# A first scan whose rows come half by DMA, half by TensorE, with stores on another queue

## The chip, the cores and the metric

The kernel runs on one core of a Trainium2 chip. The metric is the time of one execution on the device, in microseconds (us). Shapes and data are fixed. PE is TensorE (PEld its weight loads), DVE VectorE, ACT ScalarE, POOL GpSimd and SP SyncE, which here only issues DMAs.

## The reference, cut to what matters

The input is x of 32 sequences x 256 tokens x 256 channels and a condition of 32 x 512. A selective scan is followed by two layers of windowed attention and a gated feed-forward block; x is added at the end. The scan part is what the change touches:

```python
xr, gate = jnp.split(x @ W_in.T, 2, axis=-1)
xr = xr + t_emb[:, None, :]
xc = silu(causal_conv4(xr) + b_conv)
xn = layernorm(xc) * ln_g + ln_b                  # 512 channels
Bm, Cm, dt = jnp.split(xn @ W_xproj.T, 3, axis=-1)  # 16 states each
Ad = 1.0 + tanh(dt @ W_dt.T + b_dt) * 0.01 * (-tanh(A_log))
Bd = Bm * jnp.minimum(norm(xn), 1.0)
h = clip(h * ad[:, :, None] + bd[:, :, None] * xt[:, None, :], -10, 10)  # each token
yt = einsum('bd,bdh->bh', ct, h)
y = ys + D * xn
out = (y * silu(gate)) @ W_out.T
```

Here h has 16 states x 512 channels for each sequence, and a step depends on the step before.

## The kernel before

All data is fp32, apart from a mask and a scratch in bf16. The 32 sequences are worked in four groups of eight (`GB`). `program` runs the scan of group 0 by itself, then, for each group, attention and feed-forward of that group (`blocks`) side by side with the scan of the next group; `side_by_side` (L61) deals out `SCAN_PIECES` pieces of the scan over the main pieces. The last group has no scan beside it.

`group_scan` (L304) keeps h as a tile of 128 partitions (16 states x 8 sequences) by 512 channels. The 256 tokens are cut in eight chunks (`NCH`) of 32 (`CH`), and a chunk in two halves of 16 tokens (`TB`), called hb. The decay is taken out of the recurrence: by running products, a step is one add with two clamps on DVE (`step`, L550). Its other operand is row t of xn, repeated for all 16 states and scaled by a per-partition beta:

- `norm_out` (L456) stores the normalised tokens, by SP, to a scratch in DRAM, `xnd`.
- `load_rows` (L536) reads two rows (`XR` = 2) of it back, each repeated 16 times over the partitions, into a tile `xrep` of 512 KB. There are three such tiles.
- `scale_row` (L541) multiplies one row in place by beta on ACT (L543).
- `step` adds it to h. There are eight h tiles.
- `read_out` (L557) contracts the states on PE with weights `ly`, four tokens into four strips of 32 columns (`NQ` = 4), into a PSUM bank `y` for each half.
- `load_skip` (L570) reads the same 16 tokens of `xnd` again, not repeated, in four DMAs into `xd`: partition 32q + 8i + b holds token 4i + q of sequence b. `skip` (L582) multiplies by D on POOL, `gated` adds y, `out_turn` transposes on PE, `out_gate` multiplies by the gate, `project_y` projects, `copy_y` evacuates on ACT and `put_y` (L648) stores to the scratch `ys`, by SP.
- `raw_turn` (L403) takes raw B, C and dt sums from a tile of 64 partitions to one of 128, in three DMAs by SP.

Order is written out as an agenda: `at(s, what, ...)` puts a piece into slot s, slot c*32 + t being that of step t of chunk c, and every slot is emitted in the order of its list. The tile framework then orders each engine's instructions and places the waits; the order in the trace is near that of the slots, not the same. [...] Seven PSUM banks (`ps_w`) are shared, in turn, by all products but y. Slots before the change, relative to a chunk's first step s0: `load_x` -46, `project` of the convolution's half -40 to -34 and of the gates 13, 16, 17, 18, `raw_turn` -23, `norm_stats` -22 and -18, `norm_out` -17 and -13, `load_rows` five slots and `scale_row` two slots ahead of a step, `read_out` four tokens at a time one or two slots after the last of them, `load_skip` 5 and 21, `skip` 9 and 25, `put_y` 42 and 44.

Of the kernel before, what the change touches and what calls it, by code (L numbers as in the profile page):

```python
# [10 lines left out]
FP = mybir.dt.float32  # L11
BF = mybir.dt.bfloat16
I32 = mybir.dt.int32
AF = mybir.ActivationFunctionType
# [5 lines left out]
P = 128  # L20
# [3 lines left out]
DI = 512  # L24
NC_ = DI // P
NS = 16
GB = 8
CH = 32
NCH = S // CH
TB = P // GB  # L30
NQ = 4
NI = TB // NQ
NJ = GB * CH // P
BJ = GB // NJ
XR = 2
TAPS = 4
HEADS = 8
DH = 64
# [14 lines left out]
def bc(ap, axis, n):  # L53

    ap = ap.unsqueeze(axis)
    shape = list(ap.shape)
    shape[axis] = n
    return ap.broadcast_to(shape)
# [15 lines left out]
def kernel(  # L74
# [29 lines left out]
    nc = tc.nc  # L104
# [23 lines left out]
    dskip_sb = loaded(d_skip.partition_broadcast(P), [P, DI], "dskip_sb")  # L128
# [8 lines left out]
    ident = const.tile([P, P], FP, tag="ident", name="ident")  # L137
    make_identity(nc, ident)

    def sums(name, n, src):  # L140
        t = const.tile([P, n], FP, tag=name, name=name)
        nc.vector.tensor_reduce(t, src, AX.X, ALU.add)
        return t
# [2 lines left out]

    st_seq = sums("st_seq", GB, ident.rearrange("p (n b) -> p b n", b=GB))
    tok_step = sums("tok_step", CH, ident.rearrange("p (b t) -> p t b", b=BJ))

    sel = const.tile([P, NJ, NS, GB], FP, tag="sel", name="sel")  # L150
    nc.gpsimd.memset(sel, 0.0)
    tok_seq = sums("tok_seq", BJ, ident.rearrange("p (b t) -> p b t", b=BJ))
    for j in range(NJ):
# [25 lines left out]
        out=mask_t[:, 0:W], in_=mask_t[:, 0:W], compare_op=ALU.is_ge, fill=MASKED_LOW,  # L179
# [3 lines left out]
        out=mask_t[:, W : 2 * W], in_=mask_t[:, W : 2 * W], compare_op=ALU.is_ge,  # L183
# [9 lines left out]
    for h in range(HEADS):  # L193
# [7 lines left out]
        out=b1g_sb[DH : DH + MREM], in_=b1[0:MREM, :, 1, len(MCH) - 1]  # L201
# [12 lines left out]
    with tc.tile_pool(name="setup", bufs=2) as setup, tc.tile_pool(  # L214
        name="setup_ps", bufs=2, space=PSUM
    ) as sps:

        for src, pos, dst in ((qk_scale, rot_c, rc_sb), (qk_scale_sw, rot_s, rs_sb)):
            tab = setup.tile([P, NW, 2, DH], FP, tag="tab", name="tab")
            nc.scalar.dma_start(out=tab, in_=pos)  # L220
            for l in range(L):
                sc = setup.tile([P, 2 * DH], FP, tag="qk_sc", name="qk_sc")
                nc.scalar.dma_start(
                    out=sc, in_=src[l].rearrange("a d -> (a d)").partition_broadcast(P)
# [39 lines left out]
        for i in range(3):  # L264
            for src, k, dst in ((wx_sb, 0, wsum), (wx0, 1, wbias)):
# [3 lines left out]
                for c in range(NC_):  # L269
# [4 lines left out]
                        start=(c == 0),  # L274
                        stop=(c == NC_ - 1),
# [7 lines left out]
    for i in range(2):  # L283
        t = const.tile([P, NI * (P + GB)], FP, tag=f"ly{i}", name=f"ly{i}")
# [3 lines left out]
    def program(ctx, exact):  # L288
        rpool = ctx.enter_context(tc.tile_pool(name="res", bufs=1, reuse_waits="tile"))
        wpool = ctx.enter_context(tc.tile_pool(name="weights", bufs=1, reuse_waits="tile"))  # L290
        sp = ctx.enter_context(tc.tile_pool(name="sp", bufs=1, reuse_waits="tile"))
# [5 lines left out]
        ap_ = ctx.enter_context(tc.tile_pool(name="at", bufs=2, reuse_waits="tile"))  # L297
        aw = ctx.enter_context(tc.tile_pool(name="aw", bufs=3, reuse_waits="tile"))
        ps_w = ctx.enter_context(tc.tile_pool(name="psw", bufs=7, space=PSUM, reuse_waits="tile"))

        def bank(pool, tag, name):
            return pool.tile([P, DI], FP, tag=tag, name=name)

        def group_scan(g, ys):  # L304
# [2 lines left out]

            b0 = g * GB  # L310
            agenda = {}
            state = {"p": one}
            ck = [{} for _ in range(NCH)]

            def at(s, what, *args):
                agenda.setdefault(s, []).append(partial(what, *args))
# [86 lines left out]
            def raw_turn(c):  # L403
                rw = sm.tile([P, 3, CH], FP, tag="rw", name="rw")
                raw = ck[c].pop("raw")
                for i in range(3):
                    nc.sync.dma_start(
                        out=rw[:, i],
                        in_=raw[i * NS : (i + 1) * NS].rearrange("n (b t) -> n b t", b=GB),
                    )  # L410
                ck[c]["rw"] = rw
# [121 lines left out]
            def rows(c):  # L533
                return ck[c]["xnd"].rearrange("(b t) d -> b t d", b=GB)

            def load_rows(c, t):  # L536
                xr = xp.tile([P, XR, DI], FP, tag="xrep", name="xrep")
                nc.sync.dma_start(out=xr, in_=bc(rows(c)[:, t : t + XR, :], 0, NS))
                ck[c]["rep", t // XR] = xr

            def scale_row(c, t):  # L541
                bx = ck[c]["rep", t // XR][:, t % XR]
                nc.scalar.activation(  # L543
                    bx, bx, AF.Copy, scale=ck[c]["beta"][:, t : t + 1]
                )

            def step(c, t):
# [20 lines left out]
                    )  # L568

            def load_skip(c, hb):  # L570
                xd = sp.tile([P, DI], FP, tag="xd", name="xd")
                for q in range(NQ):
                    t0 = hb * TB + q
                    nc.sync.dma_start(
                        out=xd[q * 32 : (q + 1) * 32],
                        in_=rows(c)[:, t0 : t0 + TB - NQ + 1 : NQ, :].rearrange(
                            "b i d -> i b d"
                        ),
                    )
                ck[c]["xd"] = xd  # L580

            def skip(c):  # L582
                nc.gpsimd.tensor_mul(ck[c]["xd"], ck[c]["xd"], dskip_sb)  # L583

            def gate_th(c, ch):
                th = sp.tile([P, GB * CH], FP, tag="th", name="th_g", bufs=2)
# [59 lines left out]
                ck[c]["yo", d] = yo  # L646

            def put_y(c, d):  # L648
                nc.sync.dma_start(
                    out=ys[:, d, :, c * CH : (c + 1) * CH], in_=ck[c].pop(("yo", d))  # L650
                )

            def start():
                h0 = hp.tile([P, DI], FP, tag="h", name="h0")
                nc.vector.memset(h0, 0.0)
                state["h"] = h0

            at(-1, start)
            for c in range(NCH):
                for t in range(CH):  # L660
                    at(c * CH + t, step, c, t)
            for c in range(NCH):
                s0 = c * CH

                for hb in range(CH // TB):
                    s = s0 + hb * TB
                    for i in range(NI):
                        at(s + 4 * i + 5, read_out, c, hb, i)
                    at(s + 19, gated, c, hb)
                    at(s + 22, out_gate, c, hb)  # L670
                    at(s + 9, skip, c)
                for ch in range(NC_):
                    at(s0 - 38 + 2 * ch, conv_in, c, ch)
                    at(s0 - 37 + 2 * ch, conv_taps, c, ch)
                    at(s0 - 35 + 2 * ch, conv_out, c, ch)
                for ch, s in enumerate((13, 16, 17, 18)):
                    at(s0 + s + 1, gate_th, c, ch)
                    at(s0 + s + 2, gate_out, c, ch)
                at(s0 - 24, raw_copy, c)
                at(s0 - 23, raw_turn, c)  # L680
                for j in range(NJ):
                    s = s0 - 24 + 4 * j
                    at(s + 2, norm_stats, c, j)
                    at(s + 4, norm_apply, c, j)
                    at(s + 5, norm_affine, c, j)
                    at(s + 7, norm_out, c, j)
                at(s0 - 11, length, c)
                at(s0 - 7, figures_in, c)
                at(s0 - 5, decays, c)
                at(s0 - 4, put_c, c, 0)  # L690
                at(s0 + 4, put_c, c, 1)
                for d in range(KM):
                    at(s0 + 41 + 2 * d, copy_y, c, d)
                    at(s0 + 42 + 2 * d, put_y, c, d)
            for c in range(NCH):
                s0 = c * CH
                at(s0 - 46, load_x, c)
                for ch in range(NC_):
                    at(s0 - 40 + 2 * ch, project, c, ch)
                for ch, s in enumerate((13, 16, 17, 18)):  # L700
                    at(s0 + s, project, c, NC_ + ch)
                at(s0 - 26, raw_sums, c)
                for j in range(NJ):
                    at(s0 - 24 + 4 * j, norm_turn, c, j)
                at(s0 - 9, figures, c)
                for t in range(CH):
                    if t % XR == 0:
                        at(s0 + t - 5, load_rows, c, t)
                    at(s0 + t - 2, scale_row, c, t)
                for hb in range(CH // TB):  # L710
                    s = s0 + hb * TB
                    at(s + 5, load_skip, c, hb)
                    at(s + 20, out_turn, c)
                for d in range(KM):
                    at(s0 + 39 + 2 * d, project_y, c, d)
# [3 lines left out]
                    what()  # L719
                yield  # L720

        SCAN_PIECES = NCH * CH + 46 + 13

        def load_res(ys, j):
            t = rpool.tile([P, KM, 2, 1 + S], FP, tag=f"res{j}", name=f"res{j}")
# [175 lines left out]
        class Attention:  # L901
# [52 lines left out]
            def sums(self, b):  # L954

                rs = bank(ps_w, "w", "rs")[:, 0:S]
                for kw in range(NW):
                    for r in range(2):
                        for i in range(HEADS // 2):
                            nc.tensor.matmul(  # L960
                                rs[32 * i : 32 * i + 32, kw * W :],
                                head_cols[:, r],
                                self.p[b, kw, i, r],
                                start=(kw == 0 and r == 0),
                                stop=(kw == NW - 1 and r == 1),
                            )
                rinv = aw.tile([P, S], FP, tag="rinv", name="rinv", bufs=1)
                nc.vector.reciprocal(rinv, rs)
                self.rinv = rinv
# [412 lines left out]
```

## Time and profile before

| | us |
|---|---|
| three runs | 4266.41, 4258.27, 4266.48 (median 4266.41) |
| profiled run: device time, span of its instructions | 4264.77, 4262.5 |
| first scan in the profile: first step begins, last ends | 70.6, 501.4 |

| busy, whole span | us | share |
|---|---|---|
| PE | 3885.2 | 91% |
| DVE | 2600.1 | 61% |
| ACT | 1744.2 | 41% |
| POOL | 1684.0 | 40% |

A page's slices show the busy share of 40 equal stretches in tenths. A line of a group has the source line, the engine, the tiles written and read, the shape and the number of instructions, busy us and mean ns, then the engine's idle time before them with what ended it. A line of waits has who waited for whom, the total in us, how often, and the longest. A line of the timeline has start and length in us; SPq and ACTq are DMA issues of those engines' queues; in brackets stands the idle time before, with what ended it. A wait for several things is put down to the last. One fp32 product shows as two matmul instructions.

The largest transfer by far is `xrep<-xnd`, 512 issues of 512 KB; then `xnd<-xn` 64 of 256 KB, `xd<-xnd` 256 of 64 KB, `xg<-in_xT_dram` 64 and `ys<-yo` 64 of 128 KB, `rw<-raw` 96 of 16 KB. A quarter of each belongs to the first scan.

### The profile page before, as it was taken

The page shows a single profiled execution, that of the slowest core. Times are in us where ns is not written, and L with a number is a line of the kernel's source. Part 1 is how long each engine was busy: PE and PEld are TensorE (multiplying, and loading weights), DVE is VectorE, ACT ScalarE, POOL GpSimd, SP SyncE. Part 2 cuts the span into 40 slices and gives each one's busy share as a digit, 9 for nine tenths or more (in the row PEclk, how much of TensorE's full clock was granted, in tenths as well). Part 3 has the DMA queues.
Part 4 walks back from the last instruction along what each step waited for, and adds up shares of the span by engine and source line. Part 5 has one row for each costly group of instructions (what it writes and reads, how often), then busy time and mean ns, then how long its engine had stood idle before and what let it go on. Part 6 is the DMA issues. An engine that isn't in the chain of part 4 may idle for free. (4 is left out here: it accounts for less than half of the span.)

```text
span 4262.5 us, 51606 instructions
## 1 busy us (share of the span) xinstructions
PE 3885.2 (91%) x17980; PEld 2003.9 (47%) x17980; DVE 2600.1 (61%) x4952; ACT 1744.2 (41%) x3217; POOL 1684.0 (40%) x1749
## 2 busy tenths in 40 slices
PE   5777799898898999999899999999989899999999
PEld 2222255544455445544455445554455544654653
DVE  5777557666676546766776645766677653443442
ACT  2554335443444334443444423544344433322331
POOL 3333165323553156422555126532355314523531
PEclk9899999999999999999999999999999999999999
DMA  5777603443334312443433521344333431000000
GB/s 150 178 185 180 155 24 85 119 104 105 92 92 120 100 57 56 111 108 94 115 95 96 140 67 39 85 119 104 105 95 90 127 95 51 1 20 21 1 10 31
DMA packets 266114, 386.30 MB, mean 91 GB/s; under 512 B 161779, under 2 KB 170996, under 8 KB 263668
## 3 DMA queue, kind: packets, MB, share of 16 engines
q1 hardware_dynamic: 261776, 380.86, 34.1%
q8 instruction: 145, 2.38, 0.2%
q10 hardware_dynamic: 4068, 2.04, 0.2%
q14 instruction: 125, 1.02, 0.1%
HBM read 347.70 MB, written 33.55 MB: 89 GB/s over the span
## 5 line engine op out<-in xcount | busy, mean ns | idle before, releaser
L543 ACT ACTIVATE xrep<-xrep,beta 128x512 f32<-128x512 f32 x1024 | 693.1, 715 | 929.2 <-DMA xrep<-xnd 797.2
L550 DVE CUSTOM_DVE_ANT_0 h<-h,xrep,lim 128x512 f32<-128x512 f32 x1024 | 916.4, 895 | 149.7 <-ACT xrep L543 58.5
L736 PE MATMUL ps_qkv<-wqkv_sb,res 128*128 128x512 f32 x1536 | 733.6, 616 | 16.9 <-DMA res<-ys 6.3
L760 POOL TENSOR_TENSOR rot<-rot,swp 128x512 f32<-128x512 f32 x256 | 331.1, 1293 | 586.8 <-DVE swp L757 503.5
L736 PEld LDWEIGHTS ps_qkv<-wqkv_sb,res 128*128 128x128 f32 x1536 | 287.5, 196 | 359.4 <-issue 303.3
L562 PE MATMUL y<-h,ly 128*32 128x512 f32 x2048 | 411.3, 632 | 48.9 <-DVE h L550 48.0
L768 POOL TENSOR_TENSOR rn<-ss,neg_half 128x8 f32<-128x8 f32 x256 | 434.2, 1696 | 26.5 <-DVE ss L766 14.1
L1087 PE MATMUL po_f<-ag,w_sb 128*128 128x512 f32 (+1 forms) x768 | 378.8, 617 | 37.8 <-DVE ag L1076 37.8
L752 DVE TENSOR_TENSOR rot<-ps_qkv,rc_sb 128x512 f32<-128x512 f32 x256 | 175.6, 686 | 369.2 <-ACT sq L749 369.0
L326 PE MATMUL ps_in<-xg,w_in_sb 128*128 128x256 f32 x1024 | 393.0, 517 | 1.8 <-DMA xg<-in_xT_dram 1.5
L1066 PE MATMUL pa<-hT,w_sb 128*128 128x512 f32 (+1 forms) x896 | 363.8, 596 | 0.0
L1076 DVE SCALAR_TENSOR_TENSOR ag<-pa,b_sb,gl 128x512 f32<-128x512 f32 x192 | 143.4, 747 | 329.9 <-PE pa L1066 210.3
L1066 PE MATMUL pg<-hT,w_sb 128*128 128x512 f32 x640 | 313.7, 613 | 0.0
L769 POOL TENSOR_TENSOR rot<-rot,rn 128x512 f32<-128x512 f32 x256 | 276.7, 1081 | 19.1
L326 PEld LDWEIGHTS ps_in<-xg,w_in_sb 128*128 128x128 f32 x1024 | 190.1, 199 | 187.4 <-issue 127.1
L1029 POOL TENSOR_TENSOR rstd<-ve,neg_half 128x1 f32<-128x1 f32 x128 | 76.5, 598 | 508.1 <-DVE ve L1027 494.5
L373 DVE SCALAR_TENSOR_TENSOR acc<-xr,wc_sb,acc 128x256 f32<-128x256 f32 x384 | 190.0, 506 | 126.7 <-POOL acc L362 122.7
L1087 PEld LDWEIGHTS po_f<-ag,w_sb 128*128 128x128 f32 (+1 forms) x768 | 141.6, 194 | 229.4 <-issue 143.6
L950 ACT ACTIVATE pT<-sc 128x512 f32<-128x512 f32 x384 | 206.2, 590 | 97.1 <-PE sc L941 96.4
L786 PE MATMUL ps_wo<-oT,wo_sb 128*128 128x256 f32 x1024 | 237.3, 385 | 0.0
L583 POOL TENSOR_TENSOR xd<-xd,dskip_sb 128x512 f32<-128x512 f32 x64 | 86.8, 1357 | 367.1 <-DMA xd<-xnd 202.4
L749 ACT ACTIVATE sq<-ps_qkv 128x512 f32<-128x512 f32 x256 | 148.9, 594 | 200.7 <-PE ps_qkv L736 147.5
(144 smaller groups left out, 5444.2 us busy)
## 6 DMA issues: line engine op xcount, KB each, us to landing
xrep<-xnd SPq DMA_DIRECT2D x512, 512.0 KB
xnd<-xn SPq DMA_DIRECT2D x64, 256.0 KB
xd<-xnd SPq DMA_DIRECT2D x256, 64.0 KB
wqkv_sb<-in_wqkv_dram SPq DMA_DIRECT2D x8, 1536.0 KB
w_sb<-in_w_dram SPq DMA_DIRECT2D x8, 1364.0 KB
xg<-in_xT_dram SPq DMA_DIRECT2D x64, 128.0 KB
ys<-yo SPq DMA_DIRECT2D x64, 128.0 KB
res<-ys SPq DMA_DIRECT2D x32, 256.0 KB
```

The costliest lines, as they stand in the source:

```text
L326: nc.tensor.matmul(ps, w_in_sb[:, k, ch * P : (ch + 1) * P], x, start=(k == 0), stop=(k == KM - 1),)
L543: nc.scalar.activation(bx, bx, AF.Copy, scale=ck[c]["beta"][:, t : t + 1])
L550: nc.vector._custom_dve(TENSOR_ADD_SAT, out=h_new, in0=state["h"], in1=bx, s0=ck[c]["lim"][:, 0, t : t + 1], s1=ck[c]["lim"][:, 1, t : t + 1],
L562: nc.tensor.matmul(ck[c]["y", hb][32 * q : 32 * q + 32, :], ly[hb % 2][:, 32 * t : 32 * t + 32], ck[c].pop(("h", hb * TB + t)), start=(i = ...
L736: nc.tensor.matmul(ps, res[b // 2][:, k, b % 2, t0 : t0 + W], wqkv_sb[:, k, a * DI : (a + 1) * DI], start=(k == 0), stop=(k == KM - 1),)
L760: nc.gpsimd.tensor_add(rot, rot, swp)
L768: nc.gpsimd.tensor_tensor(rn, ss, neg_half, ALU.pow)
L769: nc.gpsimd.tensor_mul(rot, rot, bc(rn, 2, DH))
L786: nc.tensor.matmul(po[:, d], wo_sb[:, c, d * P : (d + 1) * P], oT[:, c, :], start=(c == 0), stop=(c == NC_ - 1),)
L950: nc.scalar.activation(p, banks[r], AF.Exp)
L1066: nc.tensor.matmul(ps[0:n, :], self.w1[:, k, half_ * HID + o : half_ * HID + o + n], self.h[j][:, k].rearrange("p b t -> p (b t)"), start= ...
L1087: nc.tensor.matmul(self.po[d], self.w2[0:n, m, d * P : (d + 1) * P], self.ag[m][0:n, :], start=(m == 0), stop=(m == len(MCH) - 1),)
```

## The change

In the first scan (`alone`, g == 0) the rows t with t % 4 of 0 or 1 are no longer loaded 16-fold. The tile that `load_skip` fills, now `xq` (four buffers, shared with `rot` of the attention) and filled 14 slots earlier, is the moving operand of one product for each such row: `spread_rows` multiplies its 32 partitions for q = 0 or 1 by constant 0/1 weights `rep_w` of 32 rows x 128 columns, so that a bank of PSUM receives token t of all eight sequences for all 16 states. `scale_row` then reads that bank instead of `xrep` and writes the `xrep` tile, which is still taken in turn. `skip` multiplies from `xq` into a fresh `xd`. In all four scans, the DMAs of `raw_turn` and `put_y` are issued from ACT's queue, `norm_out` comes one slot later and `load_x` three slots later, and the number of scan pieces falls from 315 to 312.

```diff
+    out_row = sums("out_row", NI * GB, ident.rearrange("p (q r) -> p r q", q=NQ))
...
+            alone = g == 0
...
             def raw_turn(c):
...
-                    nc.sync.dma_start(
+                    nc.scalar.dma_start(
                         out=rw[:, i],
...
+            def by_tensor(t):
+                return alone and t % NQ < XR
+
             def load_rows(c, t):
                 xr = xp.tile([P, XR, DI], FP, tag="xrep", name="xrep")
-                nc.sync.dma_start(out=xr, in_=bc(rows(c)[:, t : t + XR, :], 0, NS))
                 ck[c]["rep", t // XR] = xr
+                if not by_tensor(t):
+                    nc.sync.dma_start(out=xr, in_=bc(rows(c)[:, t : t + XR, :], 0, NS))
+
+            def spread_rows(c, t):
+
+                xq, i = ck[c]["xq", t // TB], t % TB // NQ
+                for q in range(XR):
+                    bx = bank(ps_w, "w", "bx")
+                    r = slice(32 * q, 32 * q + 32)
+                    nc.tensor.matmul(
+                        bx,
+                        rep_w[0][r, i].rearrange("p n b -> p (n b)"),
+                        xq[r].rearrange("p h d -> p (h d)"),
+                        start=True,
+                        stop=True,
+                    )
+                    ck[c]["bx", t + q] = bx
 
             def scale_row(c, t):
                 bx = ck[c]["rep", t // XR][:, t % XR]
                 nc.scalar.activation(
-                    bx, bx, AF.Copy, scale=ck[c]["beta"][:, t : t + 1]
+                    bx, ck[c].pop(("bx", t), bx), AF.Copy, scale=ck[c]["beta"][:, t : t + 1]
                 )
...
             def load_skip(c, hb):
-                xd = sp.tile([P, DI], FP, tag="xd", name="xd")
+                if alone:
+                    xd = ap_.tile([P, HEADS, DH], FP, tag="rot", name="xq", bufs=4)
+                    ck[c]["xq", hb] = xd
+                    xd = xd.rearrange("p h d -> p (h d)")
+                else:
+                    xd = ck[c]["xd"] = sp.tile([P, DI], FP, tag="xd", name="xd")
...
+            def skip(c, hb):
+                if alone:
+                    x = ck[c]["xq", hb].rearrange("p h d -> p (h d)")
+                    ck[c]["xd"] = sp.tile([P, DI], FP, tag="xd", name="xd")
+                else:
+                    x = ck[c]["xd"]
+                nc.gpsimd.tensor_mul(ck[c]["xd"], x, dskip_sb)
...
             def put_y(c, d):
-                nc.sync.dma_start(
+                nc.scalar.dma_start(
...
+            def spread_weights():
+
+                t = aw.tile([P, NI, NS, GB], FP, tag="pT", name="rep_w", bufs=6)
+                nc.vector.tensor_copy(
+                    t, bc(out_row.rearrange("p (i b) -> p i b", i=NI), 2, NS)
+                )
+                rep_w.append(t)
...
+                at(-30, spread_weights)
...
-                    at(s + 7, norm_out, c, j)
+                    at(s + 8, norm_out, c, j)
...
-                at(s0 - 46, load_x, c)
+                at(s0 - 43, load_x, c)
...
+                    if by_tensor(t) and t % XR == 0:
+                        at(s0 + t - 4, spread_rows, c, t)
...
-                    at(s + 5, load_skip, c, hb)
+                    at(s - 9 if alone else s + 5, load_skip, c, hb)
...
-        SCAN_PIECES = NCH * CH + 46 + 13
+        SCAN_PIECES = NCH * CH + 43 + 13
```

## The prediction

> **What bounds the kernel now.** I read the page's slices first, then busy time by stage, then the groups and waits of the first scan alone, then its instructions in order of time.
>
> ```profile
> span 4262.5 us, 51606 instructions
> ...
> PE   5777799898898999999899999999989899999999
> ...
> DVE  5777557666676546766776645766677653443442
> ...
> DMA  5777603443334312443433521344333431000000
> ```
>
> A slice is 106.6 us. From the sixth on PE is 80 to 99% busy and sets the pace. In the first five (setup, then the first group's scan with nothing beside it) PE, DVE and DMA all stand near 7 and none is full: a loop of waits. That stage runs from the first scan step (L550) at 70.6 to the end of the last at 501.4, 430.8 us for 256 steps, or 53.9 us for a chunk of 32. So these windows of 54 us are about a chunk (columns: length, busy us of PE, PEld, DVE, ACT, POOL, then granted clock, DMA share, GB/s):
>
> ```profile
> 272.00:326.00 54.00, 42.95 (x140) 15.64 (x138) 42.56 (x80) 27.70 (x50) 18.93 (x25) 0.91 0.74 185
> 434.00:488.00 54.00, 45.92 (x118) 11.70 (x116) 36.63 (x59) 26.10 (x44) 4.68 (x7) 1.00 0.77 197
> ```
>
> DVE is nearest to a bound: 42.6 of 54 us. The second row is mostly the last chunk, which prepares no successor, so DVE has only 36.6. What DVE waits for, over the six chunks from 110 to 434 us, and what ACT waits for ahead of it:
>
> ```profile
> DVE h L550 <- ACT xrep L543: 31.2, 29, 2.6
> DVE stat L442 <- POOL stat L437: 13.4, 12, 1.9
> DVE xd L600 <- PE y L562: 10.8, 6, 1.8
> ...
> ACT xrep L543 <- DMA xrep<-xnd: 94.9, 52, 4.2
> ```
>
> ACT waits 94.9 us for row loads, but only 31.2 (5.2 a chunk) come through to the scan step; DVE hides the rest. All of DVE's named idle is about 71 us, 11.8 a chunk, which with 42.2 busy makes the 54. The dearest place repeats in every chunk, before step 12:
>
> ```profile
> 247.79 0.56 SPq L538 DMA_DIRECT2D xrep<-xnd  x1
> 248.75 1.87 SPq L407 DMA_DIRECT2D rw<-raw  x3
> 251.58 0.81 DVE L550 CUSTOM_DVE_ANT_0 h<-h,xrep,lim 128x512 f32<-128x512 f32 x1 [0.17 <-DVE h L550]
> 253.19 1.27 POOL L583 TENSOR_TENSOR xd<-xd,dskip_sb 128x512 f32<-128x512 f32 x1 [10.29 <-DVE st L432]
> 255.02 0.16 DVE L442 SCALAR_TENSOR_TENSOR stat<-mv,stat 128x1 f32<-128x1 f32 x1 [1.61 <-POOL stat L437]
> 255.27 0.78 ACT L446 ACTIVATE xn<-tp_x,stat 128x512 f32<-128x512 f32 x1 [3.59 <-DVE stat L442]
> 256.69 1.25 DVE L550 CUSTOM_DVE_ANT_0 h<-h,xrep,lim 128x512 f32<-128x512 f32 x1 [1.52 <-ACT xrep L543]
> ```
>
> POOL's skip (L583) holds up POOL's pow, so DVE's stat, so ACT's xn; the scaling of row 12 stands behind xn in ACT's queue, and 4.3 us pass between two steps. The three rw issues sit 1.87 us in SP's queue ahead of the next row load. Loads that met no other traffic were used 4.5 to 4.6 us after their issue began (288.22 to 292.72, 293.36 to 297.95).
>
> **What the Trainium skill says.** "TensorEngine Tiling (Array Packing)", Tiling Modes: with 32 rows by 128 columns the array is four independent tiles, and a change of mode drains it. The trace agrees on independence:
>
> ```profile
> 3655.47 1.13 PE L941 MATMUL sc<-qT,kT 64*128 64x256 f32 x8
> 3656.53 5.42 PE L736 MATMUL ps_qkv<-wqkv_sb,res 128*128 128x512 f32 x12
> ```
>
> Every fp32 product is two instructions. A whole one of N=512 takes 5.42/6 = 0.90 us; four 64-row ones of N=256 would take 4 x 0.45 = 1.8 in a row and took 1.13. Four y products in four column strips took 1.06 (250.62), not 3.6. No run shows 32 rows. "DMA: Bandwidth & Descriptors", Issuing engines are not separate DMA queues: issuing elsewhere saves only sequencer time. The trace has the same price on both: 0.33 to 0.66 us each on ACT's queue in setup, medians 0.38 (ys) and 0.59 (rw) on SP.
>
> **The change part by part.**
>
> 1. Half the row loads go: 64 of 128, 8 a chunk, 8 x 0.52 = 4.2 us of SP issue and 4.2 of some 10 MB a chunk (185 GB/s for 54 us). The other half keeps three xrep buffers: a load starts when the pair three before it has been stepped through, and has four steps of 1.0 to 1.8 us to hide 4.6 + 0.7 us (landing, scale). Light stretches will still wait. Of the 5.2 us a chunk I take off 3.5 (bounds 1 and 5.2).
> 2. skip reads xq, loaded 14 slots earlier, so it no longer waits for a landing just before POOL's pow: -1.0 a chunk (0 to -1.6, the wait on L437 shown). Rows 12 and 13 now come from PE, so their scaling may stand before xn: -1.0 more (0 to -2, what is left of the 4.3 us after DVE's own 1.2 us and the -1.0).
> 3. Spreading: 16 products of N=512 a chunk, eight pairs. Bounds for a pair: 1.06 us (the y strips) and 2.0 (two in a row, with the clock at 0.91, 2 x 0.90/0.91). I take 1.15, since the 64-row pairs overlap; 9.2 us a chunk. Room: L562 is busy 133.4 us in six chunks, 22.2 each, and eight full bursts of 1.06 are 8.5, so 13.7 us of "busy" is waiting for h; 42.9 - 13.7 + 9.2 = 38.4, under DVE's 42.5. But twice a chunk PE is the last: four slots with three gate projections (1.9 each) and y come to 6.8 us, and four with tz, raw, ps_out and y to 5.9, against some 4.6 of DVE. There a pair adds to the path; half is hidden by the two slots of lead: +1.2 a chunk (0 to +4). Behind a late spread stand y and the gates; ACT's scalings wait for it, which before waited for no PE work.
> 4. rw and ys stores move to ACT: three and two a chunk, about 3 x 0.59 + 2 x 0.38 = 2.5 us on ACT (busy 27.7 of 54), freed on SP. They wait for ACT's own copies just before; behind them stand scalings with two slots of lead: +0.3 (0 to +1). Scaling out of PSUM costs no more (L749 reads PSUM in 0.59, L543 SBUF in 0.71).
> 5. Placed at nothing: xq's four loads a half chunk are the old xd loads, same number, moved 14 slots forward on SP past row loads; at a chunk's start they wait for the xnd store (in the first chunk 2.0 us, from its issue at 59.8 to the first row load at 61.8), now a slot later, and have five slots, some 7 us, before PE needs them (0 to +1 a chunk). The weights' copy and the extra reduction, about 1 us on DVE, fall into setup, where DVE is busy 21.6 of 60 us. load_x three slots later avoids SP standing behind the gate projection (8.0 us of L339 waits from 60 to 500), but its two xg issues then meet other loads: 0 (-0.5 to +0.5).
>
> Sum a chunk: -3.5 - 1.0 - 1.0 + 1.2 + 0.3 = -4.0; seven chunks -28. The last chunk (48.7 us, 452.7 to 501.4) is bound by loads, 3.0 us a pair; with every second load gone I take 5 us for four rows instead of 6.1: -9. Later groups: the groups of PE show 228 us of idle time from 560 to 3600 and 10 us after it, when no scan runs; only ys and rw leaving SP can shorten that (by the issue times, row loads start some 15 us a group late behind them), and 40 ACT issues a group cost some of it: -4 (-20 to +20, the order of all queues may shift). Total -41 on the span of 4262.5 (device time of that run 4264.8); the three runs lie at 4258.3 to 4266.5, and against their median of 4266.4 this is **4225**.
>
> **Rivals.**
> *DVE and POOL hold the pace anyway.* From 276 to 297 DVE lost 1.0 us to rows while ACT waited 10.6. If PE's new work eats what the loads give back, only the last chunk gains: 4266 - 9 + 5 = 4262.
> *The whole loop opens.* If DVE's idle falls from 11.8 to 3 a chunk: 7 x 8.8 + 12 = 74, giving 4192. For it: every stall before step 12 and in the last chunk begins at a load. Against: pow, y and the gates stay.
> *PE becomes the bound (slower).* If 32-row pairs do not overlap and each switch drains, a pair costs 2 us, 16 a chunk; on 42.9 busy this is 58.9 against 54, +4.9 x 8 = +39: 4305. It decides from 1.4 us a pair, (54 - 42.9)/8, if none of the waiting inside y can be filled because y stands in order. xq landing late would look the same: spread, y and gates all wait on it, so the change would do half of what it says.
>
> **How the numbers follow.** A measurement here tells about 0.2%, 8.5 us, from no change. Main case 0.55, open loop 0.15, no change 0.15, PE-bound 0.15. The main case with its bounds spans 4200 to 4255; with the open loop below and half of no change and PE-bound above, the range is 4188 to 4270. Faster 0.72, same 0.13, slower 0.15.
>
> **What would show it.** Right: DMA share in these windows near 0.45 and L538 with 64 loads in the first scan; DVE's wait on xrep under 2 us a chunk; DVE 42 of about 50 us; a pair of spread products near 1.15 us; last step near 464; PE idle from there on as before. Wrong: spread pairs at 2 us, PE near full in the scan, ACT waiting for bx instead of DMA, or the later groups moving by more than 20 us.

## The result, and the profile after

The median of four runs of each kernel is 4263.9 us before (4258.3 to 4266.5) and 4219.3 us after (4213.0 to 4222.7); the ratio is 0.990, with a 95% interval of 0.988 to 0.991. The profiled spans are 4262.5 and 4211.2 us, so 51.3 us have gone from the profile. Of these, 21.7 lie in the first scan, whose last step now ends at 479.7 us instead of 501.4, and 29.6 in all that follows (span less the end of the first scan: 3761.1 before, 3731.5 after). The prediction had put 37 and 4 there. Its total fits by luck: two errors cancel, and the experiments below are about both. The profiled execution of after (4213.0 us) is the fastest of its four, that of before (4264.8) is not, so that some 7 us of the 51.3 may lie in the choice of the execution.

In the page of the kernel after, the first lines and slices:

```profile
span 4211.2 us, 51779 instructions
...
PE   6888899899999999899989999889989999999999
...
DVE  5888556676676546666677636767667654433442
...
DMA  4433313444335312344333521344433531000000
```

In slices two to five DMA has come down from 6 or 7 tenths to 3 or 4, and PE and DVE have both gone up from 7 to 8. The same by windows (length, busy us of PE, PEld, DVE, ACT, POOL, granted clock, DMA share, GB/s), a middle stretch and the last chunk:

```profile
272.00:326.00 54.00, 45.67 (x172) 17.97 (x164) 43.37 (x81) 26.22 (x48) 20.72 (x25) 0.85 0.40 107
434.00:479.00 45.00, 43.76 (x157) 13.00 (x150) 35.08 (x50) 24.32 (x42) 4.38 (x6) 0.81 0.46 111
```

PE is busy 45.7 of 54 us (43.0 before), DVE 43.4 (42.6), and PE's granted clock is 0.85 where it was 0.91. In the last stretch PE is busy 43.8 of 45 us. What DVE, ACT and PE wait for in the six chunks from 110 to 434 us:

```profile
DVE st L437 <- PE tp_x L427: 15.8, 6, 3.2
DVE h L574 <- ACT xrep L567: 7.2, 9, 1.2
```

```profile
ACT xrep L567 <- DMA xrep<-xnd: 52.1, 31, 3.8
```

```profile
PE tz L639 <- DVE xd L633: 39.6, 6, 6.6
PE ps_st L483 <- DVE rhs L482: 8.3, 6, 1.4
PE y L586 <- DVE h L574: 1.8, 5, 0.8
```

The step's wait for rows fell from 31.2 to 7.2 us. In its place DVE waits 15.8 us for PE's transposes (`tp_x`), a wait that was not among its larger ones before. PE no longer waits inside `y` for the next state (32.7 us in this stretch before, 1.8 now): the room that the prediction found in `y` is filled. One long wait is left to PE, once a chunk: the transposes `tz` wait for DVE's `xd`, as they did before (35.2 us).

What follows that wait is slow too. PE's timeline around one of them:

```profile
288.74 1.11 PE L639 MATMUL tz<-ident,xd 128*128 128x128 f32 x4 [6.61 <-DVE xd L633]
289.79 2.08 PE L556 MATMUL bx<-xq,rep_w 32*128 32x512 f32 x4
291.79 1.94 PE L586 MATMUL y<-h,ly 128*32 128x512 f32 x8
293.66 3.68 PE L397 MATMUL ps_raw<-xc,wx_sb 128*64 128x256 f32 x8
...
299.19 1.13 PE L556 MATMUL bx<-xq,rep_w 32*128 32x512 f32 x4
```

The spread pair takes 2.08 us just after the idle time and 1.13 ten microseconds later; `y` takes 1.94 against 1.06 elsewhere. The granted clock has the same pattern (columns as above):

```profile
290.00:298.00 8.00, 8.00 (x23) 2.84 (x24) 6.38 (x8) 3.09 (x6) 1.78 (x1) 0.55 0.37 96
299.00:307.00 8.00, 8.00 (x44) 3.58 (x43) 5.54 (x9) 5.50 (x10) 2.66 (x3) 1.00 0.51 103
```

The granted clock is 0.55 from 290 to 298 and 1.00 from 299 on. The Trainium skill, "TensorE: Matmul & The Clock Gate", Part 1: The HAM clock gate, says that TensorE falls back to half its clock after about 3.4 us without work and needs about 3.4 us of work to be given it back. For this wait the trace agrees on the first part (6.6 us idle, then half); the slow stretch is longer here, from 288.7 to about 297. The kernel before shows the same at the same place, in the trace that the prediction was made from:

```profile
243.22 1.12 PE L606 MATMUL tz<-ident,xd 128*128 128x128 f32 x4 [5.80 <-DVE xd L600]
244.26 1.94 PE L562 MATMUL y<-h,ly 128*32 128x512 f32 x8
```

Elsewhere the trace differs from the skill on both parts. Earlier in the same chunk of after, the clock falls after a much shorter wait:

```profile
265.37 0.43 PE L483 MATMUL ps_st<-rhs,sel 128*128 128x96 f32 x2 [1.43 <-DVE rhs L482]
```

The granted clock is 0.50 from 268 to 272, and a pair's products take 2.07 us. The like wait before the last chunk (1.45 us, at 429.1) is followed by a granted clock of 0.50 from 432 to 450 us, though PE is busy 17.0 of these 18 us.

### The profile page after: what moved, and what is told of

Its sections match the earlier page's. It is cut to its first block, busy times and chain, and to the rows that moved or that the text cites. A ratio compares the mean times of both kernels' runs of the same rounds, so it can differ in the third digit from the quotient of the medians.

```text
span 4211.2 us, 51779 instructions
## 1 busy us (share of the span) xinstructions
PE 3891.7 (92%) x18236; PEld 2021.5 (48%) x18236; DVE 2605.8 (62%) x4954; ACT 1747.0 (41%) x3217; POOL 1709.8 (41%) x1749
## 5 line engine op out<-in xcount | busy, mean ns | idle before, releaser
L574 DVE CUSTOM_DVE_ANT_0 h<-h,xrep,lim 128x512 f32<-128x512 f32 x1024 | 936.0, 914 | 105.3 <-PE y L586 29.2
L567 ACT ACTIVATE xrep<-xrep,beta 128x512 f32<-128x512 f32 x896 | 613.1, 716 | 824.9 <-DMA xrep<-xnd 695.0
L331 PE MATMUL ps_in<-xg,w_in_sb 128*128 128x256 f32 x1024 | 401.5, 526 | 22.2 <-DVE res L840 10.3
L1133 PE MATMUL po_f<-ag,w_sb 128*128 128x512 f32 (+1 forms) x768 | 367.8, 602 | 5.0 <-DVE ag L1122 5.0
L586 PE MATMUL y<-h,ly 128*32 128x512 f32 x2048 | 324.7, 646 | 4.4 <-DVE h L574 4.2
L815 POOL TENSOR_TENSOR rot<-rot,rn 128x512 f32<-128x512 f32 x256 | 276.7, 1081 | 19.2
L987 PE MATMUL sc<-qT,kT 64*128 64x128 f32 (+1 forms) x2048 | 227.7, 352 | 0.0
```

Source lines behind the costliest of these rows:

```text
L331: nc.tensor.matmul(ps, w_in_sb[:, k, ch * P : (ch + 1) * P], x, start=(k == 0), stop=(k == KM - 1),)
L567: nc.scalar.activation(bx, ck[c].pop(("bx", t), bx), AF.Copy, scale=ck[c]["beta"][:, t : t + 1])
L574: nc.vector._custom_dve(TENSOR_ADD_SAT, out=h_new, in0=state["h"], in1=bx, s0=ck[c]["lim"][:, 0, t : t + 1], s1=ck[c]["lim"][:, 1, t : t + 1],
L586: nc.tensor.matmul(ck[c]["y", hb][32 * q : 32 * q + 32, :], ly[hb % 2][:, 32 * t : 32 * t + 32], ck[c].pop(("h", hb * TB + t)), start=(i = ...
L815: nc.gpsimd.tensor_mul(rot, rot, bc(rn, 2, DH))
L987: nc.tensor.matmul(banks[r][:, i, :], kT[rows, i0 + i, kw * W : (kw + 1) * W], qT[rows, i0 + i, kw * W :], start=False, stop=(i == n - 1),)
```

## The experiments

Every ratio is to the kernel before, run on the same chip, with its 95% interval; that of the kernel after is 0.990. "Scan end" is the end of the last step of the first scan in the profile, "rest" the span less it. Both are read from one execution, and executions of one kernel differ by up to 27 us (e3: 4241.5 to 4268.5), so the ratios are firmer than the split. How far these repeat: kernels with the same first scan ended it at 479.7 and 474.2, and kernels with the same later groups had rests within 3 us (before and the first run below) and within 17 us (five kernels with the pieces of after).

| kernel | median us | ratio | scan end | rest |
|---|---|---|---|---|
| before | 4263.9 | 1 | 501.4 | 3761.1 |
| after | 4219.3 | 0.990 [0.988, 0.991] | 479.7 | 3731.5 |
| e1 spreading only | 4241.9 | 0.9945 [0.993, 0.996] | 481.9 | 3758.2 |
| e2 queues only | 4266.8 | 0.9992 [0.998, 1.000] | 520.4 | 3745.4 |
| e3 slots only | 4257.9 | 0.998 [0.997, 0.9985] | 515.2 | 3736.8 |
| e10 load_x slot only | 4255.6 | 0.9965 [0.995, 0.998] | 513.4 | 3738.3 |
| e5 queues and slots | 4270.6 | 1.001 [1.000, 1.002] | 528.9 | 3741.1 |
| e4 spread twice | 4266.4 | 1.000 [0.999, 1.001] | 521.0 | 3743.8 |
| e7 a quarter spread | 4222.0 | 0.990 [0.988, 0.992] | 478.8 | 3733.4 |
| e6 idle filled | 4197.0 | 0.983 [0.982, 0.985] | 460.5 | 3748.0 |
| e8 later turn, 314 pieces | 4238.3 | 0.994 [0.992, 0.996] | 464.3 | 3768.8 |
| e11 later turn and fill | 4218.8 | 0.988 [0.987, 0.990] | 478.6 | 3737.9 |
| e9 315 pieces | 4181.3 | 0.9795 [0.978, 0.981] | 474.2 | 3704.6 |
| e12 fill and 315 pieces | 4173.3 | 0.977 [0.975, 0.978] | 459.1 | 3713.6 |

**e1: the spreading alone.** The kernel after, with the stores of `raw_turn` and `put_y` back on SP (the first two lines, in both functions) and the old slots:

```diff
-                    nc.scalar.dma_start(
+                    nc.sync.dma_start(
-                    at(s + 8, norm_out, c, j)
+                    at(s + 7, norm_out, c, j)
-                at(s0 - 43, load_x, c)
+                at(s0 - 46, load_x, c)
-        SCAN_PIECES = NCH * CH + 43 + 13
+        SCAN_PIECES = NCH * CH + 46 + 13
```

> Only the spreading by TensorE in the first scan (with xq loaded earlier); stores stay on SP, norm_out and load_x in their old slots. Theory A (two separate gains): the first scan's last step ends near 480 as with the whole change (501 before), the later groups are as before, so about 22 us faster than before, near 4242. Rival B (the spreading is worth little by itself, the freed SP queue is what helps): under 8 us faster. Rival C (the spreading carries the later groups as well): 40 us faster or more.

The scan ends at 481.9 and the rest is before's within 3 us. The spreading gives the first scan its gain and nothing else.

**e2 and e3: the queues alone, the slots alone.** Both start from the kernel before; e2, in `raw_turn` and in `put_y`:

```diff
-                    nc.sync.dma_start(
+                    nc.scalar.dma_start(
```

> Only the DMAs of raw_turn and put_y move from SP's queue to ACT's, in all four scans. Theory A: the 30 us that the later groups gained come from SP's queue being free of waits for ACT, so 20 to 35 us faster than before, all of it after the first scan, which stays at 501 within 6 us. Rival B: the later gain comes from the later norm_out and load_x, and this changes less than 8 us. Rival C: the issues on ACT cost more than they free, 5 to 15 us slower.

e3:

```diff
-                    at(s + 7, norm_out, c, j)
+                    at(s + 8, norm_out, c, j)
-                at(s0 - 46, load_x, c)
+                at(s0 - 43, load_x, c)
-        SCAN_PIECES = NCH * CH + 46 + 13
+        SCAN_PIECES = NCH * CH + 43 + 13
```

> Only norm_out one slot later, load_x three slots later, 312 pieces for 315. Theory A: within 8 us of before. Rival B (the later slots are what the later groups gained from, since SP stands less before the loads): 20 to 30 us faster than before, with a group cycle of 1000 us for 1010.

Each shortens the rest, by 15.7 and 24.3 us, and each gives much or all of it back in a first scan that loads all rows by DMA: 19.0 and 13.8 us later. That loss was not expected. e2's total is the one that its rival B named (under 8 us), but as the sum of a gain and a loss; e3's 10 us lie between its two theories.

**e10: which of the slots.** e3 without the change of `norm_out`:

```diff
-                at(s0 - 46, load_x, c)
+                at(s0 - 43, load_x, c)
-        SCAN_PIECES = NCH * CH + 46 + 13
+        SCAN_PIECES = NCH * CH + 43 + 13
```

> The kernel before with load_x at -43 and 312 pieces, and nothing else; norm_out stays at +7. If the later groups' gain of the two slots together (24 us) is that of the number of pieces and load_x, it is here in full, 18 to 30 us, and if norm_out's later slot is what cost the first scan 14 us, that scan now ends within 5 us of before's 501: the kernel at 0.993 to 0.996 of before. If norm_out's slot carried the gain, the later groups stay within 8 us of before's.

Rest and scan end are those of e3 within 2 us. `norm_out`'s slot carries neither the gain nor, against the expectation, the loss; `load_x` with the number of pieces carries both; the loss can only be that of `load_x`, since the first scan does not use the number.

**e5: both, without spreading.** The edits of e2 and e3 together.

> The kernel before with both moves (stores from ScalarE's queue, load_x at -43 and norm_out at +8) and no spreading. If the two moves gain in the later groups by themselves, whatever the first scan does, the later groups together fall by 24 to 35 us against before, as they did in the whole change (30), and the first scan, fed by DMA alone, ends 14 to 35 us later than before's 501; the sum is 0 to -15 us, a ratio of 0.996 to 1.000. The rival, that the later gain comes only because the spreading leaves something free for it, leaves the later groups at -15 or less and the kernel slower than before by 5 us or more.

The losses in the first scan nearly add (19.0 + 13.8 = 32.8; 27.5 measured), the gains in the rest do not (40.0 would be the sum, 20.0 measured). That lies between the expectation (at least 24) and the rival (at most 15). In sum there is no gain at all: without the spreading, the two moves with 312 pieces are worth nothing here. With the spreading the loss is absent: after ends its first scan at 479.7, e1 without the moves at 481.9. What makes the loss is not settled. ACT's wait for row loads from 110 to 434 us goes with it for the queues (94.9 us before, 110.0 in e2, 117.0 in e5) but hardly for `load_x` (97.8 in e10).

**e4: does PE set the pace?** The kernel after with each spread product made twice, the second over the first:

```diff
+                    for _ in range(2):
                         nc.tensor.matmul(
                             bx,
```

> The changed kernel with every spread product made twice into the same bank, so 128 products more in the first scan and nothing else. Theory A (PE sets the pace of the first scan now): eight pairs of about 1.05 us more a chunk, most of it on the path: 35 to 60 us slower than the changed kernel, near 4265. Rival B (DVE sets the pace, PE has room in its waits for h): under 15 us slower than the changed kernel, near 4225.

64 further pairs at 1.13 us are 72 us of work, and the scan ends 41.3 us later. The waits of ACT, and of DVE, from 110 to 434 us show part of it:

```profile
ACT xrep L568 <- PE bx L557: 11.6, 20, 2.1
```

```profile
DVE h L575 <- PE y L587: 13.5, 12, 2.1
```

Both were under 4 us in the kernel after (3.7 and 3.2). So over half of the added PE work lies on the path of this scan.

**e7: a quarter of the rows.** The kernel after with

```diff
-                return alone and t % NQ < XR
+                return alone and t % (2 * NQ) < XR
```

> The kernel after, with a quarter of the first group's rows spread by TensorE and three quarters by DMA. TensorE has about 47 us less to do in the first scan, DMA 33 MB/2 more to move. If TensorE sets the pace of the first scan after the change and DMA set it before, the best share lies between none and half: the first scan ends at 470 to 485, the kernel within 10 us of the kernel after on either side, faster more likely. If DMA still sets the pace at half, the quarter is slower than after by about half of the spreading's gain, 10 us or more. The later groups stay as in the kernel after in both.

The scan ends at 478.8, as with half. ACT's wait for row loads rises from 52.1 to 65.8 us in the six chunks, PE's busy time falls from 274 to 257: it seems that load time is traded for PE time at par. Half is no worse than a quarter and no better; that a quarter would more likely be faster did not come.

**e6: the idle time filled.** The kernel after, with products that nobody reads, into the bank that the transposes then overwrite (`out_turn` is handed hb for it):

```diff
                 tz = bank(ps_w, "w", "tz")
                 xd = ck[c].pop("xd")
+                for _ in range(5 if alone and hb else 0):
+                    nc.tensor.matmul(tz, ident, w_in_sb[:, 0, 0:DI], start=True, stop=True)
```

> The kernel after, with five products of 128x512 in front of the second half's out_turn of each chunk in the first scan. They are written to out_turn's own bank, which the transposes then overwrite, so they fill TensorE's idle of 5 to 6.6 us a chunk there with work that nobody needs. If the slow stretch behind that idle (the spread pair at 2.08 us for 1.13, read_out at 1.94 for 1.07, ps_raw at 3.68 for about 2.2) is what TensorE does after standing idle, and the first scan runs at TensorE's pace, then that stretch goes back to the short times and the first scan ends 10 to 25 us earlier than 480, the kernel at 0.994 to 0.998 of the kernel after. The rival: the slow stretch has another cause, or lies beside VectorE's work; then the products only delay the turn, and the kernel is 0 to 8 us slower than after.

The scan ends at 460.5, 19.2 us earlier, and the kernel is at 0.9832/0.9895 = 0.994 of after. (Its profiled run, 4210.3 us, is the longest of its five, so its rest is rather too long.) But PE's timeline shows two things at once:

```profile
275.74 3.70 PE L639 MATMUL tz<-w_in_sb,ident 128*128 128x512 f32 x8
279.37 1.13 PE L556 MATMUL bx<-xq,rep_w 32*128 32x512 f32 x4
280.43 1.51 PE L397 MATMUL ps_raw<-xc,wx_sb 128*64 128x256 f32 x6
281.87 0.66 PE L641 MATMUL tz<-ident,xd 128*128 128x128 f32 x4
282.45 1.06 PE L586 MATMUL y<-h,ly 128*32 128x512 f32 x8
```

The clock stays there (1.00 from 281 to 289; pair 1.13, y 1.06), and its mean from 110 to 434 us is 0.92 for 0.85. And the order has changed: the framework now puts the next spread pair and `ps_raw` ahead of the transposes, which find `xd` nearly done (their wait fell from 39.6 to 1.2 us in six chunks). The two were then tried apart.

**e8: the order alone.** The kernel after, its second half's turn and all that follows from it two steps later in the first scan. SCAN_PIECES, which only the later groups use, became 314 with it, which turned out to matter:

```diff
-                    at(s + 20, out_turn, c)
+                    at(s + 20 + 2 * alone * hb, out_turn, c)
...
-        SCAN_PIECES = NCH * CH + 43 + 13
+        SCAN_PIECES = NCH * CH + 43 + 15
```

(`out_gate`, `project_y`, `copy_y` and `put_y` move alike.)

> The kernel after, with the second half's out_turn, out_gate, project_y, copy_y and put_y each two steps later in the first scan, so that the next rows' spreading stands ahead of the transposes in TensorE's order and isn't held by their wait for VectorE's xd. If that wait in order is part of what TensorE loses in the first scan, the scan ends 5 to 15 us earlier than 480 and the kernel is at 0.996 to 0.999 of the kernel after; if VectorE, which does the convolution at that time, is what both wait for, no change within 5 us.

The scan ends at 464.3, 15.4 us earlier, though PE still stands idle, now before `y`, and runs slowly after it:

```profile
278.28 1.12 PE L556 MATMUL bx<-xq,rep_w 32*128 32x512 f32 x2
284.47 1.94 PE L586 MATMUL y<-h,ly 128*32 128x512 f32 x8 [5.07 <-DVE xd L633]
286.33 1.12 PE L639 MATMUL tz<-ident,xd 128*128 128x128 f32 x4
```

So most of e6's gain is to be had by a change of order alone, with no products added: the next spread rows no longer stand behind the transposes' wait. The clock changes with it, though (mean from 110 to 434 us 0.89 for 0.85, and 1.00 from 424 to 464), so the order's own share is not told apart from the clock's. The kernel as a whole is slower than after (0.994), because its rest is 37.3 us longer; the later groups' pieces are those of after, and only their number in `side_by_side` differs.

**e11: order and fill together**, with 312 pieces again. To the moves of e8, ahead of each chunk's first `read_out`:

```diff
+                if alone and i == 0 and hb == 0 and c > 0:
+                    xf = bank(ps_w, "w", "xf")
+                    for _ in range(5):
+                        nc.tensor.matmul(xf, ident, w_in_sb[:, 0, 0:DI], start=True, stop=True)
```

> The kernel after with the second half's turn two steps later in the first scan (as in the run before, but with 312 pieces) and, ahead of each chunk's first read_out, where TensorE then waits for VectorE's xd, five products of 128x512 that nobody reads. If the later turn alone gave the first scan its 15 us and the loss of that run lay in its 314 pieces alone, the later groups are at after's level, and with the idle filled the first scan ends at 450 to 462: the kernel at 4185 to 4205, at least as fast as with the idle filled alone. If the two undo the same loss, it ends near 460 all the same; if the products now delay read_out, later than 464.

The rest is back at after's level (3737.9), so e8's loss there did lie in the number 314. But the scan ends at 478.6: a miss. The products keep the clock where they stand (from 287 us on `y` takes 1.06 us and the transposes 0.66, against 1.94 and 1.12 in e8), but over the scan they do not raise it: its mean from 110 to 434 us is 0.90, against 0.89 in e8. In the last chunk it is much worse. There the clock is down when the products begin, and they take 7.5 us instead of 4.6:

```profile
440.46 7.46 PE L587 MATMUL xf<-w_in_sb,ident 128*128 128x512 f32 x10
```

```profile
420.00:446.00 26.00, 26.00 (x51) 0.50 0.36 102
```

(This window has PE's columns alone: PE is busy for all of the 26 us, at half clock. It stands after a wait of 2.63 us; in e8 a wait of 1.45 us at the same place left the clock at 1.00.) The last chunk has no convolution on DVE to wait for, so there the products can only delay: it takes 47.4 us where e8 has 39.6. That is 7.8 of the 14.3 us between the two runs; why the other chunks gained nothing is open. What the half clock costs by itself is therefore not shown: e6 took away the wait and part of the half clock together, e8 moved the wait and had less half clock too, and e11 had about as much of it as e8.

**e9: the number of pieces.** The kernel after with

```diff
-        SCAN_PIECES = NCH * CH + 43 + 13
+        SCAN_PIECES = NCH * CH + 46 + 13
```

> The kernel after with SCAN_PIECES at before's 315 instead of 312: the pieces themselves are the same, the last three are empty, and side_by_side only deals them out a little faster beside attention and feed-forward. Group 0's scan doesn't use the number, so its end stays near 480. If the gain in the later groups is a matter of which scan piece stands beside which attention piece (the run with the later turn had 314 pieces and its later groups were 35 us slower than those of the kernel after), it goes away: the later groups are 20 to 40 us slower than after, the kernel at 1.005 to 1.009 of after. If the gain comes from the moved issues and slots themselves, the number of pieces changes nothing beyond 6 us.

The number matters, and the direction was wrong: the rest falls by a further 26.9 us, to 3704.6. With the same pieces in the later groups, the rest was 3731.5 at 312, 3768.8 at 314 and 3704.6 at 315. As this first rises with the number and then falls, it is hardly a matter of faster or slower dealing but of which scan piece falls beside which piece of attention and feed-forward. It also shows that the change's step from 315 to 312 pieces lengthened the rest: e1 and e9 both have 315 and differ by the moved stores and slots alone, and their rests are 3758.2 and 3704.6. Some of PE's larger waits from 540 to 3500 us, first the kernel before, then after, then e9:

```profile
PE rs L960 <- ACT pT L950: 49.1, 20, 8.5
PE tp_hn L1044 <- DVE hn L1031: 42.6, 24, 4.6
```

```profile
PE rs L1006 <- ACT pT L996: 39.9, 13, 4.7
PE tp_hn L1090 <- DVE hn L1077: 34.4, 16, 4.6
```

```profile
PE tp_hn L1090 <- DVE hn L1077: 25.2, 7, 5.1
PE rs L1006 <- ACT pT L996: 22.0, 8, 4.2
PE tr_qk L821 <- POOL rot L815: 24.7, 7, 7.1
```

All of PE's waits there come to 216.9 us before, 188.8 in after and 170.8 in e9; that is most of the difference between the rests of these three. (It doesn't in e8: 207.3, with the longest rest.) None of them is for a DMA. The larger ones are attention's and feed-forward's own chains (softmax's sums, the norm before the feed-forward), which PE, over 90% busy there, meets earlier or later according to how many scan pieces stand between. Not all of them shrink: `tr_qk` waited for POOL's `rot` 10.3 us in after and 24.7 in e9.

**e12: the two finds together.** e6 with the edit of e9.

> The kernel after with both finds: the five unread products ahead of the second half's out_turn in the first scan, and 315 pieces. The first is worth about 19 us in the first scan, the second about 27 us in the three later groups; they lie in different stretches, so they should add: first scan near 460, later groups together near 3016, the kernel at 4155 to 4175, 0.974 to 0.978 of before. If the later groups' time is a matter of chance from build to build rather than of the number of pieces, they come back to 3043 or more and the kernel stays at 4185 to 4200.

The scan ends at 459.1, the rest is 3713.6, the ratio 0.977: as expected, and faster than both kernels (0.987 of after). That the rest at 315 pieces came back at this level in a second build speaks against chance from build to build.

## Why the prediction was right or wrong

**The total** (4225 forecast, 4219.3 measured) is right by luck, its split is not: -28 - 9 - 4 against -12.5 - 8.9 - 29.6 in the profile (first seven chunks, from the end of the first step, 381.4 to 368.9 us, last chunk 48.7 to 39.8, rest; 0.3 us is start and rounding).

1. *Loads, -3.5 a chunk:* right. The step's wait for rows fell from 31.2 to 7.2 us in six chunks, 4.0 a chunk. The DMA share is 0.40, forecast near 0.45.
2. *skip, pow and row 12, -2.0 a chunk:* the wait of `stat` for POOL (13.4 us) is gone from DVE's larger waits, as forecast. What it freed did not come through, by the next point.
3. *The step that failed first: "+1.2 a chunk" for PE.* The pair's time at full clock was right (1.13 us for 1.15). The sum of PE's work was not: 38.4 us a chunk were forecast, 45.7 came (274.15 in six chunks). The forecast counted `y` and the pairs at their full-clock times, 8.5 and 9.2 us a chunk; they took 11.4 and 12.1, at a mean clock of 0.85. Mis-sized with it is how much of PE's work lies on the path. With the other terms as forecast, seven chunks at -1.8 each leave -1.8 + 3.5 + 2.0 - 0.3 = +3.4 for PE, near the upper bound of 4. Two things had been in the trace of before and were left out: PE's wait of some 6 us a chunk for `xd`, behind which the new pairs stand (with the transposes behind the pairs, e8, the scan is 15.4 us shorter), and the half clock after it, where a pair costs 2.08. The Trainium skill states such a half clock after idle time ("TensorE: Matmul & The Clock Gate", Part 1: The HAM clock gate); the prediction did not use it. How the 3.4 us divide between the two is open. That added PE work lengthens the scan is shown by e4 (41.3 of 72 us).
4. *Stores on ACT, +0.3 a chunk, and the slots, at nothing:* for the whole change they show no cost in the first scan (479.7 with them, 481.9 without). In a scan that loads all rows they cost 19.0 and 13.8 us (e2, e3), which nothing in the prediction foresaw.
5. *The last chunk, -9:* right, 8.9.
6. *The second step that failed: later groups "-4 (-20 to +20, the order of all queues may shift)".* 29.6 us, outside the bounds. The reason given, that only `ys` and `rw` leaving SP can shorten them, is wrong: e10 gets 22.8 us with both still on SP, by `load_x` and 312 pieces, and e9 is a further 26.9 below after by the number of pieces alone. The Trainium skill, "DMA: Bandwidth & Descriptors", Issuing engines are not separate DMA queues, prices the move of an issue at sequencer time alone; e2's 15.7 us in the rest come from the moves alone, with the number of pieces unchanged, and whether they are issue time or again a shift of order these runs do not tell. In the form of the change the parts overlap, and five kernels with its pieces have rests from 3731.5 to 3748.0, so that 13 to 30 us is a fairer size than 29.6.

The rival in which PE becomes the bound had the right engine by the wrong cause: it asked for pairs of 2 us throughout, and they overlap. The rival in which DVE and POOL hold the pace forecast 4262, which did not come; but no run made DVE or POOL faster, so what they hold of it is not tested. The loop did not open by 74 us. The signs named for a wrong forecast (PE near full, later groups moving by over 20 us) are those that came.

## What to carry to other kernels

When work is added to an engine that "has room", ask where in its order the room is: here part of it lay inside `y` and was filled, but the longest wait of each chunk stood ahead of the new work, and moving the waiting transposes two steps back was worth 15 us of scan. Count products at the clock that the trace grants where they will stand, too. Where two streams are dealt onto one nearly full engine, as here, the number of pieces alone moved the time by some 30 us either way with no change of work, so that such a count is worth trying at a few values, and a gain in a stage that the change hardly touches should be tested by changing the count alone before it is given a cause. A correct total is no evidence for its terms: check each stage's share.

## What was not expected of the hardware

- PE ran at half its clock (granted clock 0.50, a pair in 2.08 us instead of 1.13) not only after a wait of 6.6 us but also after waits of 1.43 and 1.45 us; after another of 1.45 us (e8) the clock stayed at 1.00. Once down, it stayed down through 18 us in which PE was busy for 17.0 (after) and through 26 us without a pause (e11). What brings it back these runs do not tell. The mean clock from 110 to 434 us is 0.85 in after, 0.92 in e6.
- Two fp32 products of 32 rows by 128 columns on two row strips (four instructions, N = 512) take 1.13 us together at full clock, where one whole product takes 0.90.
